# Norm statistics moved from VectorE to ScalarE in a two-layer graph-attention kernel

## The chip, the cores and the metric

The kernel runs on one core of one Trainium2 chip. A core has five engines that work side by side, each through its own instructions in order: TensorE (PE: matrix products; PEld is its weight load), VectorE (DVE), ScalarE (ACT), GpSimd (POOL) and SyncE (SP, which here only issues DMAs). They wait for each other through semaphores. The metric is the time of one execution in microseconds (us) on the device, the median over several executions.

## The reference

Two graph layers over 8 batches of 2048 nodes with 256 features. Layer 0 is attention with 4 heads of 64 features, with a softmax within each chunk of 256 keys and the chunks' results added; layer 1 is an attention whose score is a sum of two node terms. Both end in a residual and a layer norm, and layer 0 has another norm inside.

```python
def _layernorm(x, axis=-1, eps=1e-5):
    m = jnp.mean(x, axis=axis, keepdims=True)
    v = jnp.var(x, axis=axis, keepdims=True)
    return (x - m) / jnp.sqrt(v + eps)

# layer 0, at its end
out = ctx @ Wo.T + bo
out = out + x
mu = jnp.mean(out, axis=-1, keepdims=True)
var = jnp.mean(jnp.square(out - mu), axis=-1, keepdims=True)
out = (out - mu) * jax.lax.rsqrt(var + EPS) * gamma + beta

# the two layers
x = _layernorm(x + _L0_gnn_ref(x, adj, ...), axis=-1)
x = _layernorm(x + _L1_gnn_ref(x, adj, ...), axis=-1)
```

So each node has three norms over its 256 features: one inside layer 0 (called `a` in the kernel), one at the end of layer 0 (`b`), one at the end of layer 1 (`c`).

## The kernel before, in words

The order of work on every engine is written out by hand. The nodes of a batch are cut into 4 groups of 512 (index `q` or `g`); a group's tile is 128 partitions by 4 rows of 256 features (`QT` is 4).

**Slots.** Layer 0's attention of one batch is 64 slots, 16 for each group of queries, also called a quarter here. In slot `s`, TensorE computes the scores of slot s+1 (L377), VectorE clips and masks them into `pr` (L388), ScalarE takes their exponential (L400), and TensorE multiplies the probabilities of slot s with the values in two products (L412), whose result ScalarE copies out of PSUM into `raw` (L419). From batch 1 on, both products use one PSUM buffer. `normalize` divides by the sums: VectorE's reciprocal `rd` (L427), GpSimd's `part` and `acc` (L434, L436).

**Layer 1 beside it.** Each slot also does three tiles of layer 1 of the batch before (`lower.step`, L796): VectorE builds `e` (L731), TensorE multiplies it (L751). A unit is 16 tiles; after its last tile the close runs one step per slot: `dn` on VectorE (L774, L775), `hh` on ScalarE (L779), `ee` and `hp` on ScalarE (L783, L785), and the write into `h1` on VectorE (L787). Batch 0's slots have no layer 1 beside them; their first part prepares the masks on VectorE and ScalarE instead.

**Between.** While the slots of group q run, group q-1 goes through the end of layer 0: bias, output projection, add, norm `a`, scale, norm `b`, then the projection for layer 1 (`values`, L563). The tables `BESIDE` and `WIDE_BESIDE` say in which slot a VectorE step is done, beside the slot's matmuls; `BEHIND` and `WIDE_BEHIND` say which ScalarE or TensorE step is done at a slot's end, behind the second product. The wide tables serve groups of quarters 1 and 2, the others quarter 3. The last group of a batch is done in the turn between two batches (L1000 to L1011).

**Closing.** Norm `c` of layer 1's result, group by group: load, add (L812), statistics, and `finish`, which applies the norm and sends the result out. From batch 2 on, the closings of the batch two before run in the first quarter's slots by the table `CLOSING`. After the last batch's slots a loop (L1040 to L1047) runs layer 1 of batch 7 alone; `CLOSING_ALONE` has batch 6's closings in it, `ENDING` batch 7's, the last two of them after the loop's last slot.

**Norm.** `stats` takes the statistics on VectorE with four `bn_stats` and four `bn_aggr`, then `rs` and `off` by two small operations on VectorE (L485, L486) and two on GpSimd (L487: the power -1/2; L488: the product). `apply` (L490) is four ScalarE instructions with `rs` as scale and `off` as bias.

Of the kernel before, what the change touches and what calls it, by code (L numbers as in the profile page):

```python
# [8 lines left out]
F32 = mybir.dt.float32  # L9
# [4 lines left out]
AF = mybir.ActivationFunctionType  # L14
ALU = mybir.AluOpType
AX = mybir.AxisListType

P = 128
# [4 lines left out]
def adj_resnorm_kernel(  # L23
# [19 lines left out]
    nc = tc.nc  # L43
    B, N, F = x.shape
# [6 lines left out]
    EPS = 1e-5  # L51
# [4 lines left out]
    QT = CH // P  # L56
# [24 lines left out]
    small = ctx.enter_context(tc.tile_pool(name="small", bufs=2))  # L81
# [71 lines left out]
    nhalf = consts.tile([P, QT], F32, tag="nhalf", name="nhalf")  # L153
# [45 lines left out]
    class Masks:  # L199
# [3 lines left out]
        def __init__(self):  # L203
            self.pieces = [
                (QT * q + u, m) for q in range(NCH) for m in range(len(BANKS)) for u in range(QT)
            ]
            self.raw, self.bits, self.done = [], [], []
            self.next = 0
# [149 lines left out]
    where = [(s // QS, s % QS // NK, s % NK) for s in range(SLOTS)]  # L358
# [79 lines left out]
    sums = {}  # L438
# [27 lines left out]
    class Norm:  # L466


        def __init__(self, src, name):
            self.src, self.name = src, name  # L470
            self.mv = small.tile([P, QT, 2], F32, tag="mv", name="mv_" + name)

        def stats(self, ks):
            sts = []
            for k in ks:
                st = small.tile([P, 6], F32, tag="st", name="st_" + self.name, bufs=4)
                nc.vector.bn_stats(st, self.src[:, k, :])  # L477
                sts.append(st)
            for k, st in zip(ks, sts):
                nc.vector.bn_aggr(self.mv[:, k, :], st)  # L480
            if ks[-1] == QT - 1:

                self.rs = small.tile([P, QT], F32, tag="rs", name="rs_" + self.name)
                self.off = small.tile([P, QT], F32, tag="off", name="off_" + self.name)
                nc.vector.tensor_scalar(self.rs, self.mv[:, :, 1], EPS, None, ALU.add)  # L485
                nc.vector.tensor_scalar(self.off, self.mv[:, :, 0], -1.0, None, ALU.mult)  # L486
                nc.gpsimd.tensor_tensor(self.rs, self.rs, nhalf, ALU.pow)  # L487
                nc.gpsimd.tensor_mul(self.off, self.off, self.rs)  # L488
# [12 lines left out]
    class Between:  # L501
# [87 lines left out]
    BESIDE = {  # L589
        1: [lambda o: o.bias()],  # L590
        4: [lambda o: o.add((0, 1))],
        5: [lambda o: o.add((2, 3)), lambda o: o.a.stats((0, 1))],
        6: [lambda o: o.a.stats((2, 3)), lambda o: o.shift()],
        8: [lambda o: o.scale()],
        9: [lambda o: o.again(), lambda o: o.b2.stats((0, 1))],
        10: [lambda o: o.b2.stats((2, 3))],
        14: [lambda o: o.turn()],
    }
    BEHIND = {
        3: lambda o: o.output((0, 1)),  # L600
        4: lambda o: o.output((2, 3)),
        7: lambda o: o.a.apply(o.y),
        11: lambda o: o.finish(),
        14: lambda o: o.values((0,)),
        15: lambda o: o.values((1,)),
# [3 lines left out]
        1: [lambda o: o.bias()],  # L609
        4: [lambda o: o.add((0, 1))],  # L610
        5: [lambda o: o.add((2, 3))],
        6: [lambda o: o.a.stats((0, 1))],
        7: [lambda o: o.a.stats((2, 3))],
        8: [lambda o: o.shift()],
        10: [lambda o: o.scale()],
        11: [lambda o: o.again()],
        12: [lambda o: o.b2.stats((0, 1))],
        13: [lambda o: o.b2.stats((2, 3))],
    }
    WIDE_BEHIND = {  # L620
        3: lambda o: o.output((0, 1)),
        4: lambda o: o.output((2, 3)),
        8: lambda o: o.a.apply(o.y),
        14: lambda o: o.finish(),
    }
    LATER_AHEAD = {0: lambda o: o.load()}
# [193 lines left out]
    class Closing:  # L820
# [5 lines left out]
        def do(self, s, beside=True, behind=True):  # L826
            for g, step in self.table.get(s, ()):
                if step == "load" and behind:
                    self.of[g] = Close(self.b, g)
                elif step == "finish" and behind:  # L830
                    self.of[g].finish()
                elif step == "add" and beside:
                    self.of[g].add()
                elif step == "stats" and beside:
                    self.of[g].n.stats((0, 1, 2, 3))


    masks = Masks()
# [6 lines left out]
    for g in range(NCH):  # L845
# [15 lines left out]

    CLOSING = {
        -1: [(0, "load")],
        0: [(0, "add"), (1, "load")],
        1: [(0, "stats")],
        2: [(0, "finish")],
        3: [(1, "add"), (2, "load")],
        4: [(1, "stats")],
        5: [(1, "finish")],
        7: [(2, "add"), (3, "load")],  # L870
        8: [(2, "stats")],
        10: [(2, "finish")],
        11: [(3, "add")],
        12: [(3, "stats")],
        13: [(3, "finish")],
    }
    CLOSING_ALONE = {
        -1: [(0, "load"), (1, "load")],
        1: [(0, "add")],
        2: [(0, "stats"), (1, "add")],  # L880
        3: [(1, "stats")],
        4: [(0, "finish"), (2, "load")],
        5: [(1, "finish"), (3, "load")],
        7: [(2, "add")],
        8: [(2, "stats"), (3, "add")],
        9: [(3, "stats")],
        10: [(2, "finish")],
        11: [(3, "finish")],
    }
    ENDING = {  # L890
        25: [(0, "load")],
        28: [(0, "add")],
        29: [(0, "stats")],
        31: [(0, "finish")],
        46: [(1, "load")],
        49: [(1, "add")],
        50: [(1, "stats")],
        52: [(1, "finish")],
        SLOTS - 1: [(2, "load"), (3, "load")],
        SLOTS: [(2, "add"), (2, "stats"), (3, "add"), (3, "stats"), (2, "finish"), (3, "finish")],  # L900
# [2 lines left out]
    for b in range(B):  # L903
# [15 lines left out]
        for s in range(SLOTS):  # L919
# [5 lines left out]
            if i == 0:  # L925
# [4 lines left out]
                if wide:  # L930
                    beside, behind = WIDE_BESIDE, WIDE_BEHIND
                else:
                    beside, behind = (BESIDE, BEHIND) if b else (BESIDE_0, BEHIND_0)
# [88 lines left out]
        else:  # L1022

            step = lower.step
# [66 lines left out]
```

## Time and profile before

| what | value |
|---|---|
| median of 4 runs | 3789.16 us (3788.06 to 3789.48) |
| the profiled execution's own time | 3789.06 us |
| its span, first to last instruction | 3787.3 us |
| mean granted TensorE clock | 0.993 |
| VectorE in L477 (bn_stats), 384 instructions | 47.0 + 46.9 + 44.7 us |
| VectorE in L480 (bn_aggr), 384 instructions | 17.4 + 17.3 + 11.5 us |
| ScalarE in L492 (apply), 384 instructions | 66.5 + 66.5 + 66.4 us |
| GpSimd in L487 and L488, 192 instructions | 151.1 + 59.7 us |
| ScalarE waiting for `pc` of L412 before L419 | 1201.3 us |

The span is shorter than the execution's time by what lies before the first and after the last instruction. An engine's busy time is the sum over the whole span; a stage with another limit is read in a window of its own. In a row of the timeline the columns are start, duration (us), engine, line, operation, output and inputs, count, and in brackets the idle time before it and what ended it. In a row of groups they are line, engine, operation, output and inputs with shapes, count, busy us, mean ns of one, then the idle time before them.

### The profile page before, as it was taken

To read this page: it belongs to the slowest core of one execution; us is meant where nothing else is said; L and a number is where in the kernel's file an instruction comes from. 1 tells how busy PE (TensorE), PEld (TensorE's weight loads), DVE (VectorE), ACT (ScalarE), POOL (GpSimd) and SP (SyncE) were. 2 spreads that over 40 slices of the span, in tenths; PEclk is the share of its full clock that TensorE was granted. 3 is DMA by queue.
4 is the path that set the end of the run, shared out by engine and by line. 5 is a ranking of instruction groups with operands and counts; after the bars stand their busy time and mean duration, and the time that the engine had idled before them with its cause. 6 is when DMAs were issued, how large, how long until landed. Compare 5 with 4: busy or idle time off the path is not lost. (4 is left out here: it accounts for less than half of the span.)

```text
span 3787.3 us, 160213 instructions
## 1 busy us (share of the span) xinstructions
PE 3677.5 (97%) x72100; PEld 2747.3 (73%) x72100; DVE 3197.0 (84%) x4810; ACT 1946.1 (51%) x3601; POOL 1387.7 (37%) x1202
## 2 busy tenths in 40 slices
PE   9999999999999999999999999999999999999787
PEld 5656677776777777776777767777677777776676
DVE  5877599977999689995999959998699968998798
ACT  4666445545555555554555545555555555555221
POOL 1445234333434243432433424443344334434310
PEclk9999999999999999999999999999999999999899
DMA  6652333333333343333433434433333334333354
GB/s 163 153 115 69 77 99 105 105 77 113 110 105 100 85 123 102 97 100 84 137 95 94 105 98 125 105 102 79 113 110 102 102 86 123 99 101 81 97 152 119
DMA packets 756545, 398.50 MB, mean 105 GB/s; under 512 B 425744, under 2 KB 721040, under 8 KB 755856
## 3 DMA queue, kind: packets, MB, share of 16 engines
q1 hardware_dynamic: 705856, 354.54, 36.2%
q10 hardware_dynamic: 50000, 33.70, 2.8%
q8 instruction: 564, 9.24, 1.0%
q14 instruction: 125, 1.02, 0.1%
HBM read 331.22 MB, written 56.89 MB: 102 GB/s over the span
## 5 line engine op out<-in xcount | busy, mean ns | idle before, releaser
L388 DVE SCALAR_TENSOR_TENSOR pr<-ps,slab 128x1024 f32<-128x1024 f32 x1024 | 1191.8, 1205 | 197.4 <-PE ps L377 195.2
L731 DVE SCALAR_TENSOR_TENSOR e<-srow,gd,et 128x640 f32<-128x640 f32 (+1 forms) x1536 | 1344.9, 932 | 10.6 <-PE pa L751 6.0
L412 PEld LDWEIGHTS pc<-vaug,pr 128*64 128x64 f32 x32768 | 1040.0, 138 | 409.9 <-issue 306.3
L412 PE MATMUL pc<-vaug,pr 128*64 128x65 f32 x32768 | 1156.5, 224 | 17.1 <-ACT raw L419 10.4
L751 PE MATMUL pa<-waug,e 128*64 128x65 f32 x32768 | 1080.9, 224 | 39.6 <-DVE e L731 38.1
L400 ACT ACTIVATE pr<-pr 128x1024 f32<-128x1024 f32 x1024 | 1044.7, 1056 | 74.0 <-DVE pr L388 63.3
L751 PEld LDWEIGHTS pa<-waug,e 128*64 128x64 f32 x32768 | 1020.1, 139 | 64.8 <-DVE e L731 38.1
L377 PE MATMUL ps<-qT,kT 64*128 64x512 f32 x4096 | 1023.6, 616 | 3.7 <-DVE pr L388 3.0
L419 ACT COPY raw<-pc 128x260 f32<-128x260 f32 x1024 | 384.7, 377 | 1230.3 <-PE pc L412 1201.3
L434 POOL TENSOR_TENSOR part<-raw,rd 128x512 f32<-128x512 f32 x448 | 468.7, 1046 | 1424.7 <-DVE rd L427 1410.4
L436 POOL TENSOR_TENSOR acc<-acc,part 128x512 f32<-128x512 f32 x448 | 575.7, 1285 | 35.1
L377 PEld LDWEIGHTS ps<-qT,kT 64*128 64x128 f32 x4096 | 350.1, 186 | 326.9 <-issue 221.6
L427 DVE RECIPROCAL rd<-raw 128x8 f32<-128x8 f32 x512 | 101.1, 197 | 100.8 <-ACT raw L419 98.9
L434 POOL TENSOR_TENSOR acc<-raw,rd 128x512 f32<-128x512 f32 x64 | 66.9, 1045 | 312.9 <-DVE rd L427 312.1
L779 ACT ACTIVATE hh<-pa,dn 128x64 f32<-128x64 f32 x512 | 114.8, 321 | 100.7 <-DVE dn L775 100.7
L571 PE MATMUL pw<-w_sb,x1T 128*128 128x264 f32 x512 | 140.0, 409 | 5.8 <-DVE x1T L283 4.7
L487 POOL TENSOR_TENSOR rs_c<-rs_c,nhalf 128x4 f32<-128x4 f32 x32 | 55.6, 1738 | 229.0 <-DVE off_c L486 229.0
L527 PE MATMUL po<-wo_sb,qT 128*128 128x256 f32 x512 | 125.5, 390 | 3.1 <-DVE qT L454 2.8
L321 PE MATMUL pp<-xT,wk_sb 128*128 128x512 f32 x256 | 119.5, 610 | 7.9 <-ACT qT L329 6.6
L321 PE MATMUL pp<-xT,wq_sb 128*128 128x512 f32 x256 | 116.2, 597 | 0.0
L337 PE MATMUL pv<-wv_sb,xT 128*128 128x256 f32 x512 | 115.9, 379 | 0.0
L571 PEld LDWEIGHTS pw<-w_sb,x1T 128*128 128x128 f32 x512 | 92.4, 193 | 27.3 <-DVE x1T L283 5.1
(93 smaller groups left out, 1856.9 us busy)
## 6 DMA issues: line engine op xcount, KB each, us to landing
et<-edgeD SPq DMA_DIRECT2D x256, 320.0 KB, 3.1
slab<-clipD SPq DMA_DIRECT2D x512, 128.0 KB, 3.2
et<-edgeD SPq DMA_DIRECT2D x128, 384.0 KB, 3.3
srow<-rowD SPq DMA_DIRECT2D x64, 320.0 KB, 4.3
xg<-in_x_dram SPq DMA_DIRECT2D x32, 512.0 KB, 5.1
x1D<-y ACTq DMA_DIRECT2D x32, 512.0 KB, 4.1
x1g<-x1D SPq DMA_DIRECT2D x32, 512.0 KB, 5.4
out_dram<-o SPq DMA_DIRECT2D x32, 512.0 KB, 3.9
```

What stands on the lines that cost most here:

```text
L321: nc.tensor.matmul(pps[c], lhsT=w[:, kc, c * P : (c + 1) * P], rhs=st["xT"][:, kc, :], start=(kc == 0), stop=(kc == KC - 1),)
L377: nc.tensor.matmul(ps[:, k, :], lhsT=kT[rows, hp, t * P : (t + 1) * P], rhs=qT[rows, hp, cols], start=True, stop=True,)
L388: nc.vector.scalar_tensor_tensor(pr, pss[u], -CLIP, slab[:, u, :].unsqueeze(1).to_broadcast([P, 2, CH]), op0=ALU.max, op1=ALU.min,)
L400: nc.scalar.activation(pr, pr, AF.Exp, scale=0.125)
L412: nc.tensor.matmul(pc[z * D : (z + 1) * D, i, :], lhsT=probs[s][u][:, k, i * P + z * D : i * P + (z + 1) * D], rhs=vaug[:, KT * c + u, 2 * ...
L419: nc.scalar.copy(raws[s][:, k], pc)
L434: nc.gpsimd.tensor_mul(part, raw[:, :, :, :D], rd.to_broadcast([P, 2, QT, D]))
L436: nc.gpsimd.tensor_add(accv, accv, part)
L527: nc.tensor.matmul(po[:, k, :], lhsT=qT[:, c, t * P : (t + 1) * P], rhs=wo_sb[:, c, :], start=(c == 0), stop=(c == KC - 1),)
L571: nc.tensor.matmul(pw[:, k, : F + 2 * H], lhsT=self.x1T[:, c, u * P : (u + 1) * P], rhs=w1_sb[:, c, :], start=(c == 0), stop=(c == KC - 1),)
L731: nc.vector.scalar_tensor_tensor(e[:, :w], self.rows[n][:, :w], self.gd[:, h, j : j + 1], self.edge[k // JG][:, j % JG, :w], op0=ALU.max, ...
L751: nc.tensor.matmul(self.pa[z * D : (z + 1) * D, i * D1 : (i + 1) * D1], lhsT=e[:, i * P + z * D : i * P + (z + 1) * D], rhs=self.waug[:, j ...
```

## The change

`Norm` gets a second way to its statistics. `sums` runs four ScalarE `Identity` activations over the group's four rows of features, each adding up its output into one column of `off`, and GpSimd makes it minus the mean. `squares` runs four `Square` activations with `off` as bias, each adding up into a column of `rs`, and GpSimd makes it the variance plus epsilon, takes the power -1/2 and multiplies `off` by it. The activations' full output goes into a tile `junk` that nobody reads.

In the slots `sums` and `squares` stand in the `BEHIND` tables and replace the two `stats` steps of the `BESIDE` tables; `shift` in the wide tables comes one slot earlier. In `CLOSING`, `CLOSING_ALONE` and `ENDING` they replace `stats`, except for the last two closings. The turn between batches keeps `stats` on VectorE.

```diff
+        def total(self, func, where, **with_bias):
+            for k in range(QT):
+                junk = small.tile([P, F], F32, tag="junk", name="junk_" + self.name, bufs=1)
+                bias = {n: t[:, k : k + 1] for n, t in with_bias.items()}
+                nc.scalar.activation(
+                    junk, self.src[:, k, :], func, accum_out=where[:, k : k + 1], **bias
+                )
+
+        def sums(self):
+            self.off = small.tile([P, QT], F32, tag="off", name="off_" + self.name)
+            self.total(AF.Identity, self.off)
+            nc.gpsimd.tensor_scalar(self.off, self.off, -1.0 / F, None, ALU.mult)
+
+        def squares(self):
+            self.rs = small.tile([P, QT], F32, tag="rs", name="rs_" + self.name)
+            self.total(AF.Square, self.rs, bias=self.off)
+            nc.gpsimd.tensor_scalar(self.rs, self.rs, 1.0 / F, EPS, ALU.mult, ALU.add)
+            nc.gpsimd.tensor_tensor(self.rs, self.rs, nhalf, ALU.pow)
+            nc.gpsimd.tensor_mul(self.off, self.off, self.rs)
...
     BESIDE = {
         1: [lambda o: o.bias()],
         4: [lambda o: o.add((0, 1))],
-        5: [lambda o: o.add((2, 3)), lambda o: o.a.stats((0, 1))],
-        6: [lambda o: o.a.stats((2, 3)), lambda o: o.shift()],
+        5: [lambda o: o.add((2, 3))],
+        6: [lambda o: o.shift()],
         8: [lambda o: o.scale()],
-        9: [lambda o: o.again(), lambda o: o.b2.stats((0, 1))],
-        10: [lambda o: o.b2.stats((2, 3))],
+        9: [lambda o: o.again()],
         14: [lambda o: o.turn()],
     }
     BEHIND = {
         3: lambda o: o.output((0, 1)),
         4: lambda o: o.output((2, 3)),
+        5: lambda o: o.a.sums(),
+        6: lambda o: o.a.squares(),
         7: lambda o: o.a.apply(o.y),
+        9: lambda o: o.b2.sums(),
+        10: lambda o: o.b2.squares(),
         11: lambda o: o.finish(),
...
     WIDE_BESIDE
-        6: [lambda o: o.a.stats((0, 1))],
-        7: [lambda o: o.a.stats((2, 3))],
-        8: [lambda o: o.shift()],
+        7: [lambda o: o.shift()],
...
-        12: [lambda o: o.b2.stats((0, 1))],
-        13: [lambda o: o.b2.stats((2, 3))],
     WIDE_BEHIND
+        5: lambda o: o.a.sums(),
+        6: lambda o: o.a.squares(),
         8: lambda o: o.a.apply(o.y),
+        11: lambda o: o.b2.sums(),
+        12: lambda o: o.b2.squares(),
         14: lambda o: o.finish(),
...
     Closing.do
+                elif step == "sums" and behind:
+                    self.of[g].n.sums()
+                elif step == "squares" and behind:
+                    self.of[g].n.squares()
...
     CLOSING = {
-        0: [(0, "add"), (1, "load")],
-        1: [(0, "stats")],
+        0: [(0, "add"), (0, "sums"), (1, "load")],
+        1: [(0, "squares")],
         2: [(0, "finish")],
-        3: [(1, "add"), (2, "load")],
-        4: [(1, "stats")],
+        3: [(1, "add"), (1, "sums"), (2, "load")],
+        4: [(1, "squares")],
         5: [(1, "finish")],
...
     CLOSING_ALONE = {
         -1: [(0, "load"), (1, "load")],
-        1: [(0, "add")],
-        2: [(0, "stats"), (1, "add")],
-        3: [(1, "stats")],
-        4: [(0, "finish"), (2, "load")],
+        1: [(0, "add"), (0, "sums")],
+        2: [(0, "squares"), (1, "add")],
+        3: [(1, "sums")],
+        4: [(0, "finish"), (1, "squares"), (2, "load")],
         5: [(1, "finish"), (3, "load")],
-        7: [(2, "add")],
-        8: [(2, "stats"), (3, "add")],
-        9: [(3, "stats")],
-        10: [(2, "finish")],
+        7: [(2, "add"), (2, "sums")],
+        8: [(2, "squares"), (3, "add")],
+        9: [(3, "sums")],
+        10: [(2, "finish"), (3, "squares")],
         11: [(3, "finish")],
     }
     ENDING = {
         25: [(0, "load")],
-        28: [(0, "add")],
-        29: [(0, "stats")],
+        28: [(0, "add"), (0, "sums")],
+        29: [(0, "squares")],
         31: [(0, "finish")],
         46: [(1, "load")],
-        49: [(1, "add")],
-        50: [(1, "stats")],
+        49: [(1, "add"), (1, "sums")],
+        50: [(1, "squares")],
         52: [(1, "finish")],
```

More of the change, by code (lines that the diff above doesn't have):

```diff
@@ L834, in do @@
                 elif step == "stats" and beside:
-                    self.of[g].n.stats((0, 1, 2, 3))
+                    self.of[g].n.stats(tuple(range(QT)))
+                elif step == "sums" and behind:
+                    self.of[g].n.sums()
+                elif step == "squares" and behind:
+                    self.of[g].n.squares()
     masks = Masks()
@@ L863, in adj_resnorm_kernel @@
         -1: [(0, "load")],
-        0: [(0, "add"), (1, "load")],
-        1: [(0, "stats")],
+        0: [(0, "add"), (0, "sums"), (1, "load")],
+        1: [(0, "squares")],
         2: [(0, "finish")],
-        3: [(1, "add"), (2, "load")],
-        4: [(1, "stats")],
+        3: [(1, "add"), (1, "sums"), (2, "load")],
+        4: [(1, "squares")],
         5: [(1, "finish")],
-        7: [(2, "add"), (3, "load")],
-        8: [(2, "stats")],
+        7: [(2, "add"), (2, "sums"), (3, "load")],
+        8: [(2, "squares")],
         10: [(2, "finish")],
-        11: [(3, "add")],
-        12: [(3, "stats")],
+        11: [(3, "add"), (3, "sums")],
+        12: [(3, "squares")],
         13: [(3, "finish")],
```

## The prediction

> **What bounds the kernel now.** The page's first part comes first, then busy time by stretch, because the stages have different limits.
>
> ```profile
> PE 3677.5 (97%) x72100; PEld 2747.3 (73%) x72100; DVE 3197.0 (84%) x4810; ACT 1946.1 (51%) x3601; POOL 1387.7 (37%) x1202
> ```
> ```profile
> core 0: us, PE busy (x) PEld busy (x) DVE busy (x) ACT busy (x) POOL busy (x), PEclk, DMA share, GB/s
> 65.40:375.20 309.80, 296.69 (x4875) 194.73 (x4873) 237.27 (x350) 207.83 (x333) 143.91 (x130) 1.00 0.50 115
> 1342.80:1734.00 391.20, 390.34 (x8778) 302.15 (x8775) 369.55 (x545) 213.99 (x395) 161.48 (x138) 1.00 0.40 107
> 3580.10:3766.90 186.80, 160.54 (x4024) 139.24 (x4026) 185.73 (x289) 35.20 (x105) 16.52 (x13) 0.94 0.49 144
> ```
>
> The rows are batch 0's slots, batch 3's slots (batches 1 to 6 look alike) and the last loop, where Layer 1 of the last batch runs alone. In batch 3 TensorE is idle for 0.86 of 391.2 us: VectorE's relief is worth nothing there. Batch 0 leaves 13.1 us idle. The last loop is the reverse: VectorE has 185.7 of 186.8 us, TensorE only 160.5. So a microsecond taken from VectorE counts in that loop, and ScalarE time counts wherever it delays somebody.
>
> The prices come from the groups by shape (busy us, mean ns of one, idle before):
>
> ```profile
> L492 ACT ACTIVATE o<-h,off_c,rs_c 128x256 f32<-128x256 f32 x128 | 66.5, 592 | 66.2 <-POOL off_c L488 66.2
> L783 ACT ACTIVATE ee<-hh 128x320 f32<-128x320 f32 x64 | 29.6, 462 | 0.3
> L582 ACT COPY sd<-pw 128x8 f32<-128x8 f32 x80 | 14.4, 180 | 0.0
> L488 POOL TENSOR_TENSOR off_c<-off_c,rs_c 128x4 f32<-128x4 f32 x32 | 28.4, 889 | 2.5
> ```
>
> **What moves.** 96 norms are computed. The 48 Between norms in the slots move, and 30 of the 32 closings; 16 norms in the turns and the last two closings stay. So 78 move. What one frees on VectorE shows in the timeline of the last loop:
>
> ```profile
> 3594.14 1.40 DVE L477 BATCH_NORM_STATS2 st_c<-h 128x6 f32<-128x256 f32 x4
> 3595.46 0.36 DVE L480 BATCH_NORM_AGGREGATE mv_c<-st_c 128x2 f32<-128x6 f32 x4
> 3595.93 0.17 DVE L485 TENSOR_SCALAR rs_c<-mv_c 128x4 f32<-128x4 f32 x1
> 3596.01 0.16 DVE L486 TENSOR_SCALAR off_c<-mv_c 128x4 f32<-128x4 f32 x1
> 3596.08 1.22 DVE L812 TENSOR_TENSOR h<-h,x1g 128x1024 f32<-128x1024 f32 x1
> ```
>
> From 3594.14 to 3596.08 that is 1.94 us a norm, 151 us in all, of which only the part in the last loop is on the path.
>
> **What a pass costs on ScalarE.** Four ACTIVATEs 128x256, each writing out its sum; neither is in the trace. The ACTIVATE: L783 falls from 511 ns (128x384) to 462 (128x320), so about 0.41 at 256; with a bias column some 0.07 more (L329, 684 ns at 512, gives 0.48). Writing the sum out costs between nothing and the shortest ScalarE row (L582, 0.18), perhaps with a wait of 0.11, as VectorE shows from L480's end to L485. Four full L492 take 2.08 where one takes 0.59, so neighbours overlap by 0.10. Low end, no read and full overlap: 4 x 0.31 + 0.10 = 1.3 us, with bias 1.6. High end, nothing overlaps and two waits per pair: 4 x 0.81 = 3.2, with bias 3.5. I take 0.55 and 0.60 per pair, a read like L582 with 0.05 hidden: **sums 2.2 us, squares 2.4 us**, nearest to the apply of 2.08. ScalarE gains 78 x 4.6 = 359 us of work.
>
> The Trainium skill speaks against the move: "ScalarE: Activation LUTs", in its rules for kernel authors, keeps adds and multiplies on VectorE. The rows agree in engine time (1.94 against 4.6 us), and by that rule alone the change would be slower everywhere; but the rule does not ask which engine is full. On the sum, "VectorE: DVE Perf Modes", in its part on two Vector instructions with no wait, counts an op with an accumulator output as two instructions; no run here shows that for ScalarE, and by it the higher half of my pass would be the likelier.
>
> **Batches 1 to 7, the slots.** The pass stands at a slot's end, behind the second `raw` copy. ScalarE's timeline there:
>
> ```profile
> 1501.93 0.38 ACT L419 COPY raw<-pc 128x260 f32<-128x260 f32 x1 [0.35 <-PE pc L412]
> 1504.98 0.38 ACT L419 COPY raw<-pc 128x260 f32<-128x260 f32 x1 [2.68 <-PE pc L412]
> 1505.26 2.01 ACT L400 ACTIVATE pr<-pr 128x1024 f32<-128x1024 f32 x2
> ```
>
> The hole is 2.68 us; 2.4 fits. Behind the pass wait that next `raw` copy and, behind it, the two exps. The copy ends at 1505.36 and the product that needs its one PSUM buffer begins at 1506.46, so it may be 1.1 us late; the exps may be 2.1 late (1507.27, product at 1509.41). Where a unit closes, hh, ee and hp take 2.36 us more over two slots. On average a first-quarter slot of 6.03 us holds 2.76 of copies and exps, 0.44 of closes and 2.4 of pass, 5.6. In quarters 2 and 3 the copies of `values` come first (0.55 us), but their matmuls lengthen the slot by 1.1. Cost **0**. High end: at 3.0 to 3.2 a pass, neighbouring passes use up the 1.1, some 0.6 to 0.9 us for one or two pairs a batch, 9 us in all.
>
> The wait that the change adds is ScalarE for `off` and for `rs` from GpSimd; one or two extra instructions of 0.2 to 1.0 us (L488 in the last loop) stand there in front of the next `part`, which has 2.33 us of work per slot of 5.7. `apply` comes one to two slots behind `squares`: in a first-quarter slot, squares 2.4 plus GpSimd 3.6 against 6.03. Just covered; if not, ScalarE stands still for some tenths of the same 1.1. SP and ScalarE's DMA issues keep their places.
>
> **Batch 0.** Quarters 2 and 3 have no Layer 1 beside them, slots take 3.93 us, and ScalarE's hole is 1.39. An apply there:
>
> ```profile
> 298.46 2.08 ACT L492 ACTIVATE y<-y,off_b,rs_b 128x256 f32<-128x256 f32 x4
> 303.36 1.97 PE L412 MATMUL pc<-vaug,pr 128*64 128x65 f32 x60 [0.38 <-ACT pr L400]
> ```
>
> With its store's issue it holds ScalarE 2.5 us and costs TensorE 0.38 idle and some 0.2 of stretching. A first pass costs about 0.3, the one directly behind it, with the slack gone, 2.4 minus 1.2, so 1.5 a quarter; the other pair stands in slots of 5 us and costs nothing. In quarter 1 VectorE carries the masks too. The four passes there cost about 0.5 each, and its four slots with statistics (5.17 to 5.44 us) come nearer to their neighbours' 4.89, which gives back about 2. Sum **+3**; ends 0 (short passes) and +8 (3.0 us and a late `part` holding `raw`).
>
> **The last loop.** Six closings save 6 x 1.94 = 11.6 us of the full engine. But ScalarE and GpSimd now form one chain, and Layer 1's closes queue in it; VectorE's L787 waits for hp. Take 0 at the end of add of group 0, three e's as 2.79 us, GpSimd 0.8 for `off`, 0.8 + 1.8 + 0.8 and handovers, 3.5, for `rs`. ScalarE: sums0 to 2.3, squares0 3.3 to 5.7, sums1 to 7.9, finish0 (rs at 9.3) to 11.5, squares1 to 13.9, finish1 (rs at 17.5) to 19.7, hh to 21.0, sums2 to 23.2, ee and hp to 24.2. VectorE reaches L787 of slot 9 at 23.25: 1.0 late. Going on: squares2 to 26.6, sums3 to 28.8, finish2 to 32.4, squares3 to 34.8, finish3 (rs at 38.4) to 40.6, hh, ee, hp to 42.9; VectorE is at slot 14's L787 at 39.0: 4.0 late. In each closing of ENDING, sums 2.2 and ee, hp 0.85 stand against three e's of 2.4: 0.85 late, twice. So 11.6 minus 6.7: **-4.9**. SP's stores wait for the later finishes, with edge loads behind them, by up to 5.7 us; those loads are needed 7.4 us after issue and land in 3.3, and the loop is then late anyway, so I add nothing. Ends: GpSimd at 0.2, 0.2, 1.2, 0.5 and passes of 1.8 give -10.9; 1.0, 1.0, 2.0, 1.0 with passes of 3.1 give +4.
>
> **Sum.** The profiled execution took 3789.06 (span 3787.3 plus 1.8 around it), the median is 3789.16. 3789.06 + 0 + 3 - 4.9 = 3787.2, say **3787**.
>
> **Rivals.**
> 1. *The chain is short.* Passes of 1.8 us and GpSimd steps near 0.2: the loop gives 10.9, batch 0 costs 1: 3779. For: the last two `off_c` of the trace took 0.20. Against: under running e's L488 takes 0.51 to 0.98. 15%.
> 2. *The pass outgrows its hole* (slower). Place: ScalarE at slot ends in all batches. Point: about 2.8 us, where a slot of 5.68 minus 2.76 and closes is used up for two slots running. At 3.0 and 3.2: slots 9, batch 0 about 7, loop +1.5: 3807. At 3.7 each of 66 neighbouring pairs (6 a batch in quarters 1 to 3 of seven batches, 4 in the first quarter of six) overruns by 2 x 0.8 less the 1.1 of slack, 33 in all; batch 0 14, loop 6: about 3842. For: an unseen read 624 times. Against: all four must run without overlap. 28%.
> 3. *Square needs another table than Exp*. The trace has one load, 1283 ns, for Exp, Identity, Copy and Relu. Two loads per squares pass are 200 us on ScalarE, half of it hidden in holes: about 3890. 2%.
>
> **Numbers.** Forecast 55%, own range 3780 to 3796. 0.2%, what a measurement here tells from no change, is 7.6 us: faster 0.15 (rival 1), within 0.55, slower 0.30 (2 and 3). Range 3778 to 3803, which leaves out most of rival 2's upper half and a little below.
>
> **What would show it.** Batch 3's slots stay at 391 us with TensorE above 390; VectorE falls by about 150 us and ScalarE rises by about 360; in the last loop 1.9 us go from each closing, and L787 waits for hp once some 4 us and three times about 1. Wrong if pairs take over 0.7 us, or if `raw` or `pr` shows up as TensorE's wait in batches 1 to 6.

## The result, and the profile after

| | before | after |
|---|---|---|
| median | 3788.39 us (61 runs) | 3793.08 us (41 runs, 3790.34 to 3795.7) |
| ratio, 95% interval | | 1.0012 [1.0008, 1.0016] |
| span of the profiled execution | 3787.3 us | 3792.0 us |

The changed kernel is 4.7 us slower: little, but the interval leaves no doubt on the sign. The time lies inside the forecast's own range and 6 us above its value, on the other side of the kernel before, so a cost is missing from the sum; that the range holds it is the width of the range and not the argument.

The page's first part of the changed kernel (busy time and share of the span, then instructions, by engine):

```profile
PE 3677.4 (97%) x72100; PEld 2744.0 (72%) x72100; DVE 3180.3 (84%) x4030; ACT 2271.2 (60%) x4849; POOL 1442.8 (38%) x1358
```

ScalarE has gained 325 us, near the 359 of the forecast. VectorE has lost 780 instructions, which took 150 us, and yet only 17 us of busy time. Where these 133 us went is the first question. Busy time by stretch of the changed kernel, for batch 0's slots, batch 3's slots and the last loop, as shown of before:

```profile
core 0: us, PE busy (x) PEld busy (x) DVE busy (x) ACT busy (x) POOL busy (x), PEclk, DMA share, GB/s
68.00:379.00 311.00, 296.27 (x4871) 194.18 (x4869) 225.16 (x288) 230.44 (x427) 149.07 (x142) 1.00 0.50 113
1348.10:1739.80 391.70, 390.46 (x8778) 302.17 (x8775) 370.58 (x444) 255.96 (x555) 167.16 (x158) 1.00 0.40 107
3586.90:3771.50 184.60, 160.09 (x4029) 137.70 (x4031) 175.52 (x230) 60.62 (x201) 26.76 (x25) 0.95 0.50 146
```

In batch 3 VectorE runs 101 instructions fewer and is busy 1.0 us longer. The last loop is 2.2 us shorter (186.8 before), although VectorE does 10.2 us less in it. The groups by shape of the changed kernel show what got slower and what the passes cost (busy us, mean ns of one, idle before):

```profile
L755 DVE SCALAR_TENSOR_TENSOR e<-srow,gd,et 128x640 f32<-128x640 f32 x1024 | 927.7, 961 | 5.4 <-PE pa L775 5.4
...
L755 DVE SCALAR_TENSOR_TENSOR e<-srow,gd,et 128x768 f32<-128x768 f32 x512 | 530.0, 1089 | 9.1 <-DMA srow<-rowD 4.6 <-DMA et<-edgeD 4.4
...
L478 ACT ACTIVATE junk_c<-h,off_c 128x256 f32<-128x256 f32 x120 | 61.3, 511 | 4.8 <-POOL off_c L485 1.9
L478 ACT ACTIVATE junk_c<-h 128x256 f32<-128x256 f32 x120 | 50.5, 421 | 24.1 <-DVE h L836 21.2
...
L478 ACT ACTIVATION_READ_ACCUMULATOR junk_c<-h 128x1 f32 x120 | 22.9, 191 | 0.0
```

The same groups before:

```profile
L731 DVE SCALAR_TENSOR_TENSOR e<-srow,gd,et 128x640 f32<-128x640 f32 x1024 | 848.2, 885 | 6.0 <-PE pa L751 6.0
L731 DVE SCALAR_TENSOR_TENSOR e<-srow,gd,et 128x768 f32<-128x768 f32 x512 | 497.3, 1026 | 4.6 <-DMA srow<-rowD 4.4
```

`e` is the same instruction on the same data, and takes 112 us more: most of the 133. (L731 of before is L755 now, L751 is L775, L785 is L809, L787 is L811, L492 is L513, L812 is L836, L818 is L842.)

The two traces can be cut at the same work: at the first `raw` copy of each batch and at the last one. What each piece gained or lost, in us, here and in the experiments told below:

| | before batch 0 | batch 0 | batches 1 to 7 | after the last slot | profiled span and median |
|---|---|---|---|---|---|
| after | +1.5 | +1.9 | +4.1 | -2.7 | +4.7; +4.7 |
| slots_only | +1.5 | +1.5 | +3.3 | -0.1 | +6.2; +7.2 |
| raw_three | +0.4 | +3.7 | +2.3 | -2.2 | +4.2; +4.8 |
| pool_later | +1.0 | +1.2 | -0.3 | -1.8 | +0.2; -2.4 |
| load_only | -0.9 | +2.7 | -0.4 | 0.0 | +1.4; +3.0 |
| tail_only | -1.1 | +1.5 | +0.4 | -1.7 | -0.9; -1.1 |

A piece whose code is that of before moves too: the piece ahead of batch 0 by -1.2 to +1.7 over all runs, an unchanged batch 0 by -0.4 to +1.5, unchanged batches 1 to 7 by -0.2 to +2.3. So a single entry means little below 1.5 us, or below 2.3 in the column of batches 1 to 7; entries that several runs share mean more. Those are +2.3 to +4.1 in batches 1 to 7 in the first three rows, and the loss of most of the 11.6 us in the last loop.

The slots of one batch alone, from its first `raw` copy to its last, scatter far less in the first two batches. Batch 1's take 387.99 us before and the same 387.99 in all six runs that change only the last loop, and also in `pool_later` and `load_only`; they take 388.98, 388.95 and 388.92 us in the changed kernel, `slots_only` and `raw_three`. (`both_mended`, with `pool_later`'s slots, has 388.20.) Batch 0's take 307.2 us before and 307.1 to 307.2 in the same six, against 309.6 in the changed kernel. So the cost in the slots is small but repeats: 0.9 to 1.0 us in batch 1, 2.4 in batch 0.

### The profile page after: what moved, and what is told of

Its sections match the earlier page's. It is cut to its first block, busy times and chain, and to the rows that moved or that the text cites. A ratio compares the mean times of both kernels' runs of the same rounds, so it can differ in the third digit from the quotient of the medians.

```text
span 3792.0 us, 160923 instructions
## 1 busy us (share of the span) xinstructions
PE 3677.4 (97%) x72100; PEld 2744.0 (72%) x72100; DVE 3180.3 (84%) x4030; ACT 2271.2 (60%) x4849; POOL 1442.8 (38%) x1358
## 5 line engine op out<-in xcount | busy, mean ns | idle before, releaser
L755 DVE SCALAR_TENSOR_TENSOR e<-srow,gd,et 128x640 f32<-128x640 f32 (+1 forms) x1536 | 1457.1, 1004 | 14.6 <-PE pa L775 5.4
L775 PE MATMUL pa<-waug,e 128*64 128x65 f32 x32768 | 1079.6, 223 | 38.4 <-DVE e L755 37.1
L775 PEld LDWEIGHTS pa<-waug,e 128*64 128x64 f32 x32768 | 1017.8, 139 | 64.5 <-DVE e L755 35.7
L434 POOL TENSOR_TENSOR part<-raw,rd 128x512 f32<-128x512 f32 x448 | 495.6, 1106 | 869.7 <-DVE rd L427 859.9
L436 POOL TENSOR_TENSOR acc<-acc,part 128x512 f32<-128x512 f32 x448 | 613.3, 1369 | 35.1
L485 POOL TENSOR_SCALAR off_c<-off_c 128x4 f32<-128x4 f32 x30 | 11.1, 371 | 267.4 <-ACT junk_c L478 264.6
```

The costliest lines, as they stand in the source:

```text
L434: nc.gpsimd.tensor_mul(part, raw[:, :, :, :D], rd.to_broadcast([P, 2, QT, D]))
L436: nc.gpsimd.tensor_add(accv, accv, part)
L755: nc.vector.scalar_tensor_tensor(e[:, :w], self.rows[n][:, :w], self.gd[:, h, j : j + 1], self.edge[k // JG][:, j % JG, :w], op0=ALU.max, ...
L775: nc.tensor.matmul(self.pa[z * D : (z + 1) * D, i * D1 : (i + 1) * D1], lhsT=e[:, i * P + z * D : i * P + (z + 1) * D], rhs=self.waug[:, j ...
```

## The experiments

**Halves.** `slots_only` has the change in the slots and the old closings in the last loop; `tail_only` has it in the last loop alone. `pool_later` keeps all passes and moves GpSimd's small steps one slot later, behind `part` and `acc`. `load_only` has ScalarE's passes in the slots and nothing else: their sums are not used, the statistics stay on VectorE.

```diff
 slots_only, against the changed kernel
-        1: [(0, "add"), (0, "sums")],
-        2: [(0, "squares"), (1, "add")],
...
+        1: [(0, "add")],
+        2: [(0, "stats"), (1, "add")],
...
 pool_later, against the changed kernel
-        6: [lambda o: o.shift()],
+        6: [lambda o: o.a.mean(), lambda o: o.shift()],
+        7: [lambda o: o.a.root()],
...
-        5: lambda o: o.a.sums(),
-        6: lambda o: o.a.squares(),
+        5: lambda o: o.a.sums(False),
+        6: lambda o: o.a.squares(False),
...
 load_only, against the kernel before
+        def sums(self):
+            spare = small.tile([P, QT], F32, tag="spare", name="spare_" + self.name)
+            self.total(AF.Identity, spare)
...
+        5: lambda o: o.a.sums(),
+        6: lambda o: o.a.squares(),
```

> The changed kernel with the old tables in the last loop: statistics there on VectorE, in the slots on ScalarE. Theory (the slots of batches 1 to 7 lose some 4 us, batch 0 some 2, the last loop gains about 3): 6 to 7 us slower than before, ratio about 1.0017. Rival (the slots are free, as predicted, and the loss lies in the last loop): within 1 us of before.

> The old kernel with the new tables in the last loop alone. Theory: about 3 us faster than before (span 3784.5 against 3787.3), VectorE there waiting some 7.6 us in all for hp and for edge loads that stand behind a late store. Rival (the loss lies here): slower than before.

> The changed kernel with GpSimd's steps of each norm in the slots issued one slot later, behind part and acc of that slot, so that these no longer wait for ScalarE; the last loop as changed. Theory (part and acc, made late by the wait, run against VectorE's e and slow it, and that delays the exps): mean e of 128x640 in the slots back from 975 to about 885 ns, batches 1 to 7 lose under 1 us, total 3 to 5 us faster than the changed kernel, so about equal to before. Rival (the passes' own time on ScalarE makes raw late): e may fall, but batches 1 to 7 keep their 4 us.

> The old kernel with the passes added on ScalarE in the slots, their sums unused, and all statistics still on VectorE; GpSimd unchanged; the last loop as before. Theory: batches 1 to 7 stay within 1 us of before in all, since a pass of 2.1 or 2.5 us fits ScalarE's hole and e stays at 885 ns; batch 0 loses 3 to 5 us. Rival (ScalarE's load alone): batches 1 to 7 lose 4 us or more.

| | median | before, same chip | ratio, 95% |
|---|---|---|---|
| slots_only | 3795.95 | 3788.79 | 1.0018 [1.001, 1.0027] |
| tail_only | 3787.67 | 3788.79 | 0.9996 [0.9988, 1.0005] |
| pool_later | 3786.37 | 3788.79 | 0.9995 [0.9986, 1.0004] |
| load_only | 3791.75 | 3788.79 | 1.0008 [0.9999, 1.0017] |

The slots' half costs 7 us, the last loop's half gives about 1, with no change inside its interval. Moving GpSimd's small steps takes the cost of the slots of batches 1 to 7 away again: `pool_later` lies below the changed kernel with intervals that don't touch, and batch 1 is back at 387.99. In `load_only`, ScalarE's whole load, without those steps, costs batches 1 to 7 nothing (batch 1: 387.99); its 3 us fit batch 0, whose slots take 310.0 us against 307.2.

How a few small steps on GpSimd do that is read from one place of batch 3. GpSimd in the changed kernel's timeline (start, duration):

```profile
1492.59 0.20 POOL L490 TENSOR_SCALAR rs_a<-rs_a 128x4 f32<-128x4 f32 x1 [2.92 <-ACT junk_a L478]
1492.87 1.04 POOL L491 TENSOR_TENSOR rs_a<-rs_a,nhalf 128x4 f32<-128x4 f32 x1
1493.98 0.70 POOL L492 TENSOR_TENSOR off_a<-off_a,rs_a 128x4 f32<-128x4 f32 x1
1494.63 1.68 POOL L434 TENSOR_TENSOR part<-raw,rd 128x512 f32<-128x512 f32 x1
1496.39 1.73 POOL L436 TENSOR_TENSOR acc<-acc,part 128x512 f32<-128x512 f32 x1
```

and VectorE at the same time:

```profile
1491.07 0.19 DVE L427 RECIPROCAL rd<-raw 128x8 f32<-128x8 f32 x1
1491.18 2.30 DVE L388 SCALAR_TENSOR_TENSOR pr<-ps,slab 128x1024 f32<-128x1024 f32 x2
1493.40 1.21 DVE L537 TENSOR_TENSOR xg<-xg,beta_sb 128x1024 f32<-128x1024 f32 x1
1494.54 4.27 DVE L755 SCALAR_TENSOR_TENSOR e<-srow,gd,et 128x640 f32<-128x640 f32 x3
1498.73 0.19 DVE L427 RECIPROCAL rd<-raw 128x8 f32<-128x8 f32 x1
```

`rd` is there at 1491.3, but `part` starts at 1494.63: GpSimd stood 2.92 us at L490 for ScalarE's squares and then did its three steps. So `part` and `acc` fall on VectorE's row of `e` instead of its `pr`, and both sides get slower: `part` 1.68 instead of 1.04 us, `acc` 1.73 instead of 1.29, the three e's 4.27 instead of 2.47. Before, the statistics were done on VectorE, GpSimd did not wait for ScalarE, and `part` and `acc` stood beside `pr`; first GpSimd, then VectorE:

```profile
1492.18 1.04 POOL L434 TENSOR_TENSOR part<-raw,rd 128x512 f32<-128x512 f32 x1
1493.31 1.29 POOL L436 TENSOR_TENSOR acc<-acc,part 128x512 f32<-128x512 f32 x1
```

```profile
1492.02 2.31 DVE L388 SCALAR_TENSOR_TENSOR pr<-ps,slab 128x1024 f32<-128x1024 f32 x2
...
1495.60 2.47 DVE L731 SCALAR_TENSOR_TENSOR e<-srow,gd,et 128x640 f32<-128x640 f32 x3
```

In `pool_later` GpSimd does `part` and `acc` as soon as `rd` is there, beside `pr` again, and its small steps after them, two of the three beside the `e`; first GpSimd, then VectorE:

```profile
1488.61 1.04 POOL L434 TENSOR_TENSOR part<-raw,rd 128x512 f32<-128x512 f32 x1 [3.06 <-DVE rd L427]
1489.73 1.29 POOL L436 TENSOR_TENSOR acc<-acc,part 128x512 f32<-128x512 f32 x1
1491.10 1.28 POOL L498 TENSOR_SCALAR rs_a<-rs_a 128x4 f32<-128x4 f32 x1
```

```profile
1488.25 0.20 DVE L427 RECIPROCAL rd<-raw 128x8 f32<-128x8 f32 x1
1488.84 2.36 DVE L388 SCALAR_TENSOR_TENSOR pr<-ps,slab 128x1024 f32<-128x1024 f32 x2 [0.38 <-PE ps L377]
...
1492.24 2.47 DVE L769 SCALAR_TENSOR_TENSOR e<-srow,gd,et 128x640 f32<-128x640 f32 x3
```

The Trainium skill has the rule behind this, in "SBUF — State Buffer", under who interferes with whom: a VectorE instruction with two inputs in SBUF contends with a GpSimd instruction that reads SBUF, and one with a single input there, outside the two-port modes, does not. The trace agrees on both: `e` reads two tiles and was slowed; `pr` reads one and PSUM, and beside it `part` and `acc` took their 1.04 and 1.29 us. The page also calls this an exclusive lock, held for a whole instruction, and the rows fit that nearly: taken one by one, the three e's last 0.87, 1.66 and 1.89 us and end at 1495.41, 1496.99 and 1498.81, with `part` and `acc` ending between them at 1496.31 and 1498.13. The engines took turns, each instruction ending 0.14 to 0.20 us sooner behind the other engine's than its time alone would have it. So all five were through in 4.27 us, where the two rows one after the other need 2.47 + 2.33 = 4.80.

How the delay gets to TensorE in the changed kernel, from ScalarE's rows and from TensorE's:

```profile
1498.75 0.38 ACT L419 COPY raw<-pc 128x260 f32<-128x260 f32 x1 [2.18 <-PE pc L412]
1500.05 2.19 ACT L400 ACTIVATE pr<-pr 128x1024 f32<-128x1024 f32 x2 [0.92 <-DVE pr L388]
...
1502.14 0.51 ACT L807 ACTIVATE ee<-hh 128x384 f32<-128x384 f32 x1
1502.56 0.51 ACT L809 ACTIVATE hp<-hh 128x384 f32<-128x384 f32 x1
1502.97 0.35 ACT L419 COPY raw<-pc 128x260 f32<-128x260 f32 x1
...
1503.38 1.15 PE L412 MATMUL pc<-vaug,pr 128*64 128x65 f32 x32 [0.41 <-ACT raw L419]
```

The long `e` makes `pr` late, the exponentials begin 0.92 us later than ScalarE could, `ee`, `hp` and the next `raw` copy queue behind them, and TensorE waits 0.41 us for PSUM; the same gap is there in each of batches 1 to 7. In batch 1 it and one of 0.28 us are the only gaps above 0.15, 0.69 of the 0.99 us; before has none there. In batches 2 to 7 before has gaps of this kind as well, of 0.34 to 0.47 us in another slot, which the change removes. Counted over the e's of 128x640 in the slots, by whether they share at least 0.3 us with an `acc`:

| | before | after | pool_later | load_only | raw_three | late_part |
|---|---|---|---|---|---|---|
| e's that meet `acc`, of 857 | 33 | 148 | 61 | 33 | 148 | 139 |
| their mean, us | 1.08 | 1.45 | 1.08 | 1.08 | 1.45 | 1.45 |
| mean of the others, us | 0.87 | 0.87 | 0.87 | 0.87 | 0.87 | 0.87 |
| e's over 1.2 us | 0 | 86 | 1 | 0 | 86 | 87 |
| TensorE's gaps above 0.15 us in the slots of batches 1 to 7, us | 14.0 | 17.0 | 13.6 | 13.8 | 15.5 | 76.5 |

**The delay alone.** `late_part` is the kernel before with one small GpSimd step, whose result nobody reads, ahead of each `part`.

```diff
+        late = small.tile([P, QT], F32, tag="late", name="late", bufs=1)
+        nc.gpsimd.tensor_tensor(late, rd[:, 0, :, 0], nhalf, ALU.pow)
         nc.gpsimd.tensor_mul(part, raw[:, :, :, :D], rd.to_broadcast([P, 2, QT, D]))
```

> The old kernel with one more GpSimd instruction in each slot, a power over 128x4 between rd and part, whose result nobody uses; nothing is added on ScalarE or VectorE. It makes part and acc 1 to 2 us later, so that acc meets VectorE's e in each slot. Theory (acc and e slow each other): mean e of 128x640 in the slots rises from 883 ns to over 1050, VectorE becomes the bound of the slots, 50 to 200 us slower. Rival (GpSimd has 60% to spare, late parts are harmless): e stays, under 3 us slower.

One run took 3892.79 us against 3789.03, 104 us more. From its groups by shape and its page's first part:

```profile
L435 POOL TENSOR_TENSOR late<-rd,nhalf 128x4 f32<-128x4 f32 x512 | 520.7, 1017 | 1292.0 <-DVE rd L427 1268.6 <-ACT sd L584 7.9 <-ACT o L494 7.8
```

```profile
PE 3707.8 (95%) x72100; PEld 2756.6 (71%) x72100; DVE 3378.4 (87%) x4810; ACT 1969.9 (51%) x3601; POOL 1993.9 (51%) x1714
```

A step of 1.02 us, no pass on ScalarE, as many long e's of 128x640 as in the changed kernel, and VectorE is busy 181 us longer with the same instructions, 148 of them in its e's of both shapes. That it costs 104 us here and 4 there fits what VectorE had in hand: in batch 3 of before it is busy for 369.6 of 391.2 us, and the change took some 20 us of statistics out of such a batch just as the long e's put some 18 back. In `late_part` nothing was taken out. That balance is worked out from the rows; no run varies it by itself.

**A buffer instead?** ScalarE's `raw` copies wait 35.1 us in all for `part` to release a buffer, 11.9 before. `raw_three` gives `raw` a third buffer, and makes `junk` bfloat16, for the room.

```diff
-            raws[s] = small.tile([P, 2, QT, D1], F32, tag="raw", name="raw")
+            raws[s] = small.tile([P, 2, QT, D1], F32, tag="raw", name="raw", bufs=3)
...
-                junk = small.tile([P, F], F32, tag="junk", name="junk_" + self.name, bufs=1)
+                junk = small.tile([P, F], mybir.dt.bfloat16, tag="junk", name="junk_" + self.name, bufs=1)
```

> The changed kernel as it is, with a third `raw` buffer (and `junk` in bfloat16, which makes the room). Theory: GpSimd's late `part` and `acc` meet VectorE's e's and slow them; buffers do not matter for that, so the slots of batches 1 to 7 stay 3 to 5 us longer than before, e 128x640 in the slots stays above 950 ns (883 before, 974 in the changed kernel), `acc` above 1.34 us, and the median is about 3792 to 3794. Rival: ScalarE's copy into `raw` has to wait for a late `part` that still reads the buffer (35.1 us of such waits in the changed kernel, 11.9 before), and that is what delays TensorE: then these waits fall below 12 us, the slots of batches 1 to 7 lose at least 3 of their 4 us with e still slow, and the median is about 3789.

Median 3794.21 against 3789.43, 1.0013 [1.0003, 1.0023]; these waits are 3.4 us, `e` is unchanged, and the time stays. Batches 1 to 7 read +2.3, below the 3 to 5 expected, and TensorE's gaps are 1.5 us fewer, so the buffer may have a small part in the later batches; in batch 1 it has none (388.92 us, and the same two gaps). The rival, which wanted the time back at about 3789, falls.

**The last loop.** Six experiments ask where its 11.6 us went. `tail_none` leaves the statistics of these six norms out (the apply uses a constant): what the work is worth with nothing in its place. `tail_tt` is `tail_only` with GpSimd's two tensor_scalar steps as tensor_tensor, and one step more for the scaling. `tail_store_act` is `tail_only` with the stores of the last two batches on ScalarE's queue instead of SP's. `tail_spread` pulls the closings apart in the tables; `both_mended` has its tables and `pool_later`'s slots. `tail_free` shortens the chain: the first pass has the scale -1/F, so GpSimd does nothing between the passes and the squares follow at once, and four of the closings and their applies stand in other slots.

```diff
 tail_store_act
-            outgoing.append(lambda: nc.sync.dma_start(out=by_node(out, self.b, self.g), in_=o))
+            if self.b < B - 2:
+                outgoing.append(lambda: nc.sync.dma_start(out=by_node(out, self.b, self.g), in_=o))
+            else:
+                nc.scalar.dma_start(out=by_node(out, self.b, self.g), in_=o)
...
 tail_spread, against the kernel before
-        1: [(0, "add")],
-        2: [(0, "stats"), (1, "add")],
-        3: [(1, "stats")],
-        4: [(0, "finish"), (2, "load")],
...
+        1: [(0, "add"), (0, "sums")],
+        2: [(1, "add"), (1, "sums")],
+        3: [(0, "squares"), (1, "squares")],
+        4: [(2, "load")],
+        5: [(0, "finish"), (1, "finish"), (3, "load")],
+        14: [(2, "add"), (2, "sums")],
...
 tail_free, against the kernel before
+            self.total(AF.Identity, self.off, scale=-1.0 / F)
...
+            nc.gpsimd.tensor_add(self.rs, self.rs, feps)
+            nc.gpsimd.tensor_tensor(self.rs, self.rs, nhalf, ALU.pow)
+            nc.gpsimd.tensor_mul(self.rs, self.rs, root)
+            nc.gpsimd.tensor_mul(self.off, self.off, self.rs)
...
-        1: [(0, "add")],
-        2: [(0, "stats"), (1, "add")],
-        3: [(1, "stats")],
+        1: [(0, "add"), (0, "sums"), (0, "squares")],
+        2: [(1, "add"), (1, "sums"), (1, "squares")],
...
+        14: [(2, "add"), (2, "sums"), (2, "squares")],
+        18: [(2, "finish")],
```

> The old kernel, whose last loop takes the statistics on ScalarE, with each closing's passes between two closes of Layer 1 and its finish behind ee and hp, so that hh, ee, hp and SP's edge loads never queue behind a pass or a late finish. Theory (11.6 us of VectorE are freed there and 8.8 us of waits take them back): VectorE's waits for hp and edge loads in the loop fall from 8.8 to under 1.5 us, and the kernel is 10 to 11.6 us faster than before, ratio about 0.9972. Rival (the freed VectorE time isn't on the path in the loop): 1 to 4 us faster, as with the new tables.

> The old kernel with the new tables in the last loop, and there each finish sends its own store from ScalarE's queue instead of SP's. Theory (SP stands at a store until its finish is done, and edge loads stand behind it): the waits of VectorE for edge loads, 4.4 us, go to under 0.5; the waits for hp, 4.4 us, grow by 0 to 2; 2 to 4 us faster than with the new tables alone, 4 to 7 faster than before. Rival (the loads are late by themselves): the waits for edge loads stay.

> The changed kernel with both repairs: GpSimd's steps of the slots one slot later, and the last loop's closings spread between the closes. Theory: batches 1 to 7 as before, the last loop 10 to 11.6 us shorter, batch 0 some 1 to 2 longer: 8 to 10 us faster than before, no better than the spread loop alone. Rival (the relief of VectorE in the slots is worth something once GpSimd is out of the way): faster than the spread loop alone.

> The old kernel, but the six closings of the last loop that the change moves leave their statistics out: finish applies a constant instead. Nothing is added anywhere. Theory (in the loop VectorE's time is the path): the loop is 11.0 to 12.5 us shorter (six blocks of 1.94), the kernel some 11.6 us faster than before, ratio about 0.9970. Rival (the freed time is mostly not on the path there): less than 5 us.

> The old kernel with the new tables in the last loop; the two GpSimd steps over 128x4 that are a tensor_scalar become a tensor_tensor with a constant tile (one step more for the scaling). Theory (that form waits until VectorE leaves its row of e's, up to 6 us): the longest GpSimd step falls from 5.7 us to under 2, the first finish starts 3 us earlier, VectorE's waits for hp and edge loads fall from 8.9 to 4 to 6 us, 4 to 7 us faster than before. Rival (any small step waits like that, the form doesn't matter): a 5 us step stays, and the waits too.

> The old kernel, the last loop on ScalarE: the mean comes scaled out of the first pass, so that squares follow at once; GpSimd's four steps are tensor_tensor; passes lie between two closes of Layer 1, finish behind ee and hp. Theory: waits for hp and edge loads under 2 us, the kernel 9 to 11.6 us faster than before, ratio about 0.9973. Rival (ScalarE and GpSimd can't do it in the room between closes): as with the spread tables alone, 0.9995.

VectorE's waits from 3580 us to the end, for `hp` and for the edge tiles `et`, beside what the piece after the last slot lost:

| | for `hp` | for `et` | waits above before | 11.6 less these | measured gain | ratio of medians, 95% |
|---|---|---|---|---|---|---|
| before | 4.3 | 0 | | | | |
| tail_none | 4.3 | 0 | 0 | 11.6 | 11.8 | 0.9971 [0.996, 0.9983] |
| after | 8.6 | 4.4 | 8.7 | 2.9 | 2.7 | |
| tail_only | 7.4 | 4.7 | 7.8 | 3.8 | 1.7 | 0.9996 [0.9988, 1.0005] |
| tail_tt | 10.4 | 4.1 | 10.2 | 1.4 | 1.2 | 1.0003 [0.9994, 1.0012] |
| tail_spread | 9.6 | 4.7 | 10.0 | 1.6 | 1.9 | 0.9995 [0.9986, 1.0004] |
| tail_store_act | 17.2 | 0 | 12.9 | -1.3 | -1.4 | 1.0008 [0.9999, 1.0017] |
| tail_free | 4.2 | 4.2 | 4.1 | 7.5 | 7.4 | 0.9983 [0.9974, 0.9991] |

(`both_mended`: 1.5 us gained in this piece, 3788.29 us against 3789.03, ratio 0.9994 [0.9985, 1.0003]; 8 to 10 us less than before was expected.) So the 11.6 us are real, and two waits account for what is missing to within 0.3 us, except in `tail_only`, where 2.1 us more are missing and 1.1 of them are a wait for TensorE's `pa`. VectorE's rows of the changed kernel show them in turn:

```profile
3620.98 1.95 DVE L755 SCALAR_TENSOR_TENSOR e<-srow,gd,et 128x768 f32<-128x768 f32 x2 [2.61 <-DMA et<-edgeD]
...
3625.74 0.56 DVE L811 SCALAR_TENSOR_TENSOR h<-ee,hp 128x384 f32<-128x384 f32 x1 [1.69 <-ACT hp L809]
...
3642.65 0.56 DVE L811 SCALAR_TENSOR_TENSOR h<-ee,hp 128x384 f32<-128x384 f32 x1 [1.59 <-ACT hp L809]
```

and GpSimd's show what stretched the chain:

```profile
3600.43 1.76 POOL L485 TENSOR_SCALAR off_c<-off_c 128x4 f32<-128x4 f32 x1 [11.64 <-ACT junk_c L478]
3604.80 5.71 POOL L490 TENSOR_SCALAR rs_c<-rs_c 128x4 f32<-128x4 f32 x1 [2.62 <-ACT junk_c L478]
3610.60 1.04 POOL L491 TENSOR_TENSOR rs_c<-rs_c,nhalf 128x4 f32<-128x4 f32 x1
```

A step on 4 columns that takes 0.20 us elsewhere took 5.71, and ended when VectorE, after nine e's back to back (3602.02 to 3610.38), came to a small instruction. Behind it ScalarE's apply stood idle 5.79 us, the store with it, and behind the store, in SP's queue, the edge loads. SP's waits for ScalarE over the last loop (us in total, times, longest), the changed kernel first, then before:

```profile
SPq L842 <- ACT o L513: 30.5, 6, 7.2
```

```profile
SPq L818 <- ACT o L492: 3.8, 4, 1.8
```

SP stood 30.5 us at the stores (before: 3.8), and the loads came too late for VectorE. `tail_store_act` shows that this is the edge waits' cause: with the stores elsewhere they are 0. But the kernel got no faster, since VectorE's waits for `hp` then grew, to 6.9 and 5.0 us: VectorE came sooner to a late chain, and the chain was longer too. From the slow step's start to the end of the first `hp` it took 23.4 us, 20.9 in the changed kernel; each store's issue ahead of `hh` holds ScalarE 0.5 us there. `tail_tt` refutes that the tensor_scalar form makes the step slow: as tensor_tensor it took 5.75 us. `tail_spread` was expected to free the loop and did not; its rows show both first applies behind the same slow step (6.07 us there). `tail_free`, without a GpSimd step between the passes and with the last four applies three to five slots behind their adds, has no wait for `hp` beyond those of before. Its GpSimd rows at that place:

```profile
3597.39 1.07 POOL L492 TENSOR_TENSOR rs_c<-rs_c,feps 128x4 f32<-128x4 f32 x1 [14.25 <-ACT junk_c L481]
3598.53 1.66 POOL L493 TENSOR_TENSOR rs_c<-rs_c,nhalf 128x4 f32<-128x4 f32 x1
3600.27 0.98 POOL L494 TENSOR_TENSOR rs_c<-rs_c,root 128x4 f32<-128x4 f32 x1
```

No step is held up for long here, though VectorE runs its e's and adds as well; what decides when one is, stays open. No run takes the slow step out and leaves the rest as it was, so its share in the waits for `hp` is read from the rows and not shown by an experiment of its own.

**A version ahead of both.** `tail_free` is the slots of before and the new statistics in the last loop alone: 3781.2 us against 3788.15, 0.9983 [0.9974, 0.9991]. It gains 7 us of the 9 to 11.6 expected; the 4.2 us of edge waits left in it were not tried.

## Why the prediction was wrong, point by point

- **The price of the passes: right.** A pair is an ACTIVATE of 0.42 us (0.51 with bias) and a read of 0.19, one pair every 0.54 (0.64) us: sums 2.13 and squares 2.5 us, against 2.2 and 2.4. The read exists, overlaps a little, and takes what L582 takes. So rival 2 did not come about.
- **Batches 1 to 7, "Cost 0": this step failed.** ScalarE's part of it holds (`load_only`). What failed is the sentence on GpSimd, where extra instructions stand "in front of the next `part`, which has 2.33 us of work per slot of 5.7". It asked whether GpSimd has the time, and GpSimd has. It did not ask beside which VectorE instruction `part` and `acc` then run. Besides, it counted the steps and not the wait in front of them: GpSimd takes its queue in order, and stood up to 3 us for ScalarE with `part` behind. In its place: 148 instead of 33 e's of 128x640 beside an `acc`, 112 us more of `e`, and +4.1 us (+3.3 and +2.3 in the two runs with the same slots). The sign that the prediction named for being wrong, `raw` as TensorE's wait, came with it; the other one, 391 us for batch 3 with TensorE above 390, was too coarse to see 0.5 us a batch.
- **VectorE falls by about 150 us: wrong for the same reason.** It fell by 17. TensorE's 390 us in batch 3 hold (390.46 of 391.70); there, relief of VectorE was worth nothing, as said, and `pool_later`, which keeps all of it, gains nothing in the slots.
- **The last loop, -4.9: right sign, mis-sized.** Its gross 11.6 us is confirmed by `tail_none`. The chain's waits for `hp` were put at 6.7 and are 4.3. The GpSimd step was put at 0.8 and was 5.7 where it hurt. The edge loads, where the text says "I add nothing", cost 4.4; their reason, that the loop is late anyway by then, was wrong. Net -2.7.
- **Batch 0, +3: right.** Its slots take 2.4 us more in the changed kernel, and 1.4 to 3.9 more in the six runs with passes there. `pool_later`, with 1.4, and `load_only`, with 2.9, are among them, so ScalarE's passes alone cost it something, as forecast.
- **The other rivals.** No table was loaded for Square: the one load of 1283 ns is the only one here too. Rival 1 needed passes of 1.8 us, which took 2.13 and 2.5, and GpSimd steps near 0.2, which took 0.2 to 5.7. The slower case given had its place on ScalarE; the real one was on GpSimd and VectorE, and is not among the rivals.

The sum's 0 in batches 1 to 7, +3 in batch 0 and -4.9 at the end are by measurement 2 to 4, 2.4 and -2.7, so 2 to 4 us in all where the forecast had -1.9; the medians differ by 4.7. The rest is of the size of the scatter of single profiles and is not put down to anything.

## What to carry to other kernels

When a step is put into an engine's queue, count the wait it brings for whatever stands behind it, and look beside which instruction of the other engines that will then run: a transfer or an elementwise step that was hidden may be moved from a harmless neighbour onto one that it slows. A relief on an engine that bounds one short stage is best made in that stage alone, with the shortest chain that can do it; here the change outside that stage only cost. And where a result is stored from a queue that also issues loads, a later result makes the loads late.

## What the chip showed that was not expected

- VectorE's `e` (128x640 f32, all operands in SBUF) takes 0.87 us alone and 1.45 on average where it meets GpSimd's `acc` in the changed kernel; `acc` rises from 1.285 to 1.37 us on average and up to 2.34.
- A GpSimd step of 128x4 took from 0.19 to 2.75 us, but one step of the last loop took 5.70 to 6.07 in eight of the runs, while VectorE ran e's of 128x768 back to back, as tensor_scalar and as tensor_tensor alike.
- An activation with an accumulator output is two instructions on ScalarE: at 128x256, 421 ns (511 with a bias column) and 190 ns for the read, together one per 0.54 (0.64) us.
